# Whole tiled blocks, output stores from ScalarE, and ten early x in a four-layer graph kernel

## The chip, the core and the metric

The kernel runs on one core of a Trainium2 chip. The core has five engines with an instruction stream each: PE (TensorE, the matrix unit), DVE (VectorE), ACT (ScalarE), POOL (GpSimd) and SP (SyncE, which here only issues transfers). An instruction starts when the one before it on its engine is through and the semaphores it waits for are set; engines do not look past a waiting instruction. The metric is the device time of one execution in microseconds (us), less is better. The profile comes from one such execution.

## The reference, cut to what matters

The input `x` holds 128 independent batches of 128 nodes with 512 features (float32). Each batch goes through four layers, and after each one `x = layernorm(x + layer(x))`, without gain or bias:

```python
# 0: x1 = (adj @ x) @ W0 + bias0
# 1: h = x @ W;  e = leaky_relu(h@a1 [rows] + h@a2 [columns]) * adj
#    layer = elu(softmax(e) @ h + beta * h)
# 2: A = adj @ x;  layer[o] = max over columns of relu(A + b[o])
# 3: q, k, v = x @ w_qkv  (8 heads of 64)
#    o = softmax(q k^T / 8, masked where adj == 0) @ v,  then o @ w_proj + b_proj
#    layer = o + layernorm(o) * gamma + beta3
```

In layer 2 both weight matrices of the general form are `adj`, so the pairwise term falls away and the line above is what is left of it.

## The kernel before, in words

The work is planned in Python while the program is built. Each batch is a chain, a generator called `batch(i)` (L1009 in the profile's numbering), which asks for an engine with `yield use(engine, work, take, late, urgent, follow)`: how long it will need it, which buffers it takes, how much later the result is there. `Plan.run` (L161) always grants the request that could start first by these estimates; among equals, `follow` goes ahead of `urgent`, and that ahead of the rest, then the lower rank, which is the batch number less some head start. When a request is granted, the chain goes on and writes its instructions. So the order on every engine is fixed at build time by the planner's estimates; on the chip each engine only follows its list. A request counts as able to start when its engine is free and its buffers are given back (`at`, L126). `yield event` makes a chain wait without an engine.

Buffers are few. PSUM has eight banks, `ps`. In SBUF there are 21 buffers `t` of 512 columns, 15 `q` of 1024 and 7 `u` of 256. `CAPS` limits how many of them one use may hold: 8 `x`, 2 `xr`, 4 `yT` (all `t`), 4 `v`, 8 `qk` and 4 `xT` (all `q`).

Batches form groups of four (the last two groups have two). In order, a batch is loaded (`load`, L402), mixed by the adjacency (L300 for the first 12, L319 through a transposition by DVE and a round trip through DRAM `x_d` for the others), multiplied by W0 (L292), normalised, and given attention logits; `attention1` (L649) makes the attention weights of two batches at a time with two more round trips (`s_d`, `e_d`). Then come layer 1 (L300 with `u`, and seven half-size products per pair of batches instead of eight, L832), layer 2 (L1096) and a transposition through `x_d`. For a group of four, `section` (L860) makes q, k and v of all its batches, again in seven products each (L881). A batch that waits for its turn is spilled to DRAM (`x_s`, L998) and fetched again (L1006), since x buffers are short.

Two steps use the matrix unit in halves, the *tiled* steps. `score` (L952) makes the 8 heads' logits of one batch: eight matmuls over 64 rows, in pairs that run side by side, into two PSUM banks. The banks come free when DVE has added the mask to them (two instructions L1128). `attends` (L973) multiplies v by the transposed softmax: eight matmuls with 64 columns each into one bank, which comes free when ACT has copied it (L1192). `tiled` (L927) writes, for one group, its own four scores and the four attends of the group before. Three scores are one request that takes six banks; the fourth score and the four attends are single requests with `follow=True`. Between two requests other work on PE can be granted. The last `APART = 5` groups take no attends with them; these are requests of their own (`attend`, L965).

After `attends` a batch is projected (seven products per pair, L832; the last four batches with L292 or L1304), and `normed` (L1269) adds, normalises and stores it: the last step before the store is the activation L279 on ACT, and the store is issued by SP (L1287).

At the start `loads` (L431) issues adjacency, weights and the first x in a fixed order. Batches 0 to 7 have x buffers; `GUESTS = 6` more, 8 to 13, lie two each in the three first `v` buffers, which the first group doesn't need yet. The others wait for an x buffer.

Near the end, three numbers shift ranks: `LAST, AHEAD` move the last 14 batches 8 ranks ahead, and `SOON` moves the q, k, v and tiled requests of the last six groups ahead by up to 20.

Of the kernel before, what the change touches and what calls it, by code (L numbers as in the profile page):

```python
# [19 lines left out]
APART = 5  # L20
FIRST = 0
PAIRS = 2
SOON = 0,4,8,12,16,20
WHOLE = 2
KEPT = 4
ATTENDS = 2
# [1 line left out]
SEVEN1 = 1  # L28
SEVENP = 1
PLAIN = 4  # L30
GUESTS = 6
CLOSE = 2900
SOFT = 10
PROJ = 0
# [11 lines left out]

BUFS = {"ps": 8, "t": 21, "q": 15, "u": 7}
POOL = {"x": "t", "xr": "t", "yT": "t", "v": "q", "qk": "q", "xT": "q"}
CAPS = {"x": 8, "xr": 2, "yT": 4, "v": 4, "qk": 8, "xT": 4}
LAST,AHEAD = 14,8  # L50
DIRECT = 12
LATER = 2
LANDED = 4.0
# [15 lines left out]
class Plan:  # L69
# [9 lines left out]
    def __init__(self):  # L79
        self.free, self.requests = {}, []  # L80
        self.slots = {name: [0.0] * n for name, n in BUFS.items()}
        self.caps, self.held = {name: [0.0] * n for name, n in CAPS.items()}, {}
        self.now = 0.0

    def use(self, engine, work, take=None, late=0.05, urgent=False, follow=False):

        names = take if callable(take) else lambda: (take,) if take else ()
        return engine, work, names, late, 0 if follow else 1 if urgent else 2
# [4 lines left out]
    def done(self, event, late=0.0):  # L97
        event.left -= 1
        event.at = max(event.at, self.now + late)
        if not event.left:  # L100
            for r in event.chains:
                r["ready"] = max(r["ready"], event.at)
                self.step(r, None)

    def give(self, slot):
        name, i = slot
        self.slots[POOL.get(name, name)][i] = self.now
        if name in CAPS:
            self.caps[name][self.held.pop(slot)] = self.now
# [51 lines left out]
    def run(self):  # L161
        while self.requests:
            t, _, _, n = min(
                (self.at(r), r["want"][4], r["rank"], n) for n, r in enumerate(self.requests)
            )
            assert t < float("inf"), "the chains wait for each other"
            r = self.requests.pop(n)
            engine, work, take, late, _ = r["want"]
            self.free[engine] = t + work
            self.now = r["ready"] = t + work + late  # L170
            got = self.claim(take())
            self.step(r, got[0] if len(got) == 1 else got)
# [3 lines left out]
def gnn_stack_kernel(  # L176
# [17 lines left out]
    nc = tc.nc  # L194
    NB = x.shape[0]
# [5 lines left out]
    ps = ctx.enter_context(tc.tile_pool(name="ps", bufs=1, space=PSUM))  # L201

    plan = Plan()
    use, give, done = plan.use, plan.give, plan.done
# [197 lines left out]
    def load(i, engine="SP", queue=nc.sync):  # L402
        n = i - CAPS["x"]
        if 0 <= n < GUESTS:
            slot = yield use(engine, 0.5, () if n % 2 else "v")
            x_slot[i] = x_slot[i - 1] if n % 2 else slot
            if not n % 2:
                room[slot] = buf(slot, 2, D)
                guests[slot] = 2
            xs[i] = room[x_slot[i]][:, n % 2]  # L410
        else:
            x_slot[i] = yield use(engine, 0.5, "x")
            xs[i] = buf(x_slot[i], D)
        queue.dma_start(xs[i], x[i])
        landing(loaded[i], P)
# [15 lines left out]
    def loads():  # L431
        yield use("SP", 0.4)
        adj_slot.append((yield use("SP", 0.0, "t")))
        adj_sb = buf(adj_slot[0], D)[:, :P]
        adj_slot.append(adj_sb)
        nc.sync.dma_start(adj_sb, adj)
        landing(adj_in, P // 4)
        yield from load(0, "ACT", nc.scalar)
        w0_slot.extend((yield use("SP", 0.0, lambda: ("qk", "qk"))))
        halves = [buf(slot, 2, D) for slot in w0_slot]  # L440
        w0_nat.extend(halves[k // 2][:, k % 2] for k in range(K))
        for k in range(K):
            yield use("SP", 0.4)
            nc.sync.dma_start(w0_nat[k], w0[k * P : (k + 1) * P])
            landing(w0_chunk[k], P)
        yield from load(1)
        yield use("SP", 0.4)
        nc.sync.dma_start(bias0_sb, rows(bias0, D))
        landing(bias0_in, P)
        for i in range(2, 4):  # L450
            yield from load(i)
        slot = yield use("SP", 1.0, "qk")
        matrix(w1_sb, w1)
        a_sb = buf(slot, 2, D)
        nc.sync.dma_start(a_sb, rows(a, 2 * D).rearrange("p (s f) -> p s f", s=2))
        landing(w1_in, (K + 2) * P)
        plan.start(logit_rows(a_sb, slot), 0)
        for i in range(4, 8):
            yield from load(i)
        yield use("SP", 2.0)  # L460
        permuted(w0_sb, w0)
        landing(w0_in, K * P)
        yield use("SP", 1.0)
        nc.sync.dma_start(beta1_sb, rows(beta1, 1))
        nc.sync.dma_start(
            b2_sb, bass.AP(tensor=b2.tensor, offset=b2.offset, ap=[[1, P], [1, 1]])
        )
        landing(scalars_in, 2 * P)
        for i in range(8, CAPS["x"] + GUESTS):
            yield from load(i)  # L470
        yield use("SP", 2.5)
        permuted(wqkv_sb, w_qkv)
        matrix(wproj_sb, w_proj)
        for dst, src in ((bproj_sb, b_proj), (gamma_sb, gamma), (beta3_sb, beta3)):
            nc.sync.dma_start(dst, rows(src, D))
        landing(w3_in, (4 * K + 3) * P)
        plan.start(weight_sums(), 0)
        for i in range(CAPS["x"] + GUESTS, NB):
            yield from load(i)

    idle = []
# [140 lines left out]
    def soon(g):  # L622
        return SOON[g - len(sizes)] if g >= len(sizes) - len(SOON) else 0

# [302 lines left out]
    def tiled(gr, before, bs):  # L927
        yield gr.qk
        waiting = list(range(before.size)) if before else []
        for b in waiting:  # L930
            yield before.rows[b]

        now, later = bs[:3], bs[3:]
        slots = yield use(
            "PE", 0.45 + 0.87 * len(now) + (0.1 if waiting else 0),
            lambda: ("ps", "ps") * len(now), late=0.0, urgent=True,
        )
        for b in now:
            score(gr, b, slots[:2])
            slots = slots[2:]  # L940

        for n, b in enumerate(now):
            done(gr.scored[b], 0.15 - 0.87 * (len(now) - 1 - n))
        for b in later:
            slots = yield use("PE", 0.87, lambda: ("ps", "ps"), late=0.0, follow=True)
            score(gr, b, slots)
            done(gr.scored[b], 0.15)
        for b in waiting:
            slot = yield use("PE", 0.87, "ps", late=0.0, follow=True)
            attends(before, (b,), [slot])  # L950

    def score(gr, b, slots):  # L952

        p = [bank(slot, K, P) for slot in slots]
        qk = gr.qkT[b]
        for c in range(K):
            for j in range(2):
                rws = slice(j * HD, (j + 1) * HD)
                nc.tensor.matmul(
                    p[j][:, c, :], qk[rws, c, :], qk[rws, K + c, :],  # L960
                    start=True, stop=True,
                )
        gr.sc[b] = p, slots
# [9 lines left out]
    def attends(gr, bs, slots):  # L973
        for b, slot in zip(bs, slots):
            v, prT = gr.heads.pop(b)

            p = bank(slot, K, P)
            for c in range(K):
                for j in range(2):
                    nc.tensor.matmul(  # L980
                        p[j * HD : (j + 1) * HD, c, :],
                        v[:, (2 * c + j) * HD : (2 * c + j + 1) * HD],
                        prT[:, j * K + c], start=True, stop=True,
                    )
            give(gr.slot["qk", b])
            gr.o[b] = p, slot, v
        for n, b in enumerate(bs):
            done(gr.attended[b], 0.2 - 0.87 * (len(bs) - 1 - n))
# [280 lines left out]
    def normed(i, o, release, fetched):  # L1269

        added = yield from add_rows(o, fetched, i)
        xb = xs[i]
        mv, rstd = yield from mean_rstd(o)
        yield added
        b_t1 = yield use("DVE", 2.0, "t")
        t1 = buf(b_t1, D)
        nc.vector.scalar_tensor_tensor(  # L1277
            t1, o, mv[:, 0:1], gamma_sb, op0=ALU.subtract, op1=ALU.mult
        )
        total = row_sums()  # L1280
        nc.vector.scalar_tensor_tensor(  # L1281
            xb, t1, rstd, xb, op0=ALU.mult, op1=ALU.add, accum_out=total[0]
        )
        release()
        yield from layernorm_sums(xb, total, b_t1)
        yield use("SP", 0.5, late=3.0)
        nc.sync.dma_start(out[i], xb)  # L1287
        give(x_slot[i])

    def last(i, oT, v, release, biased):  # L1290
# [100 lines left out]
```

## Time and profile before

| | us |
|---|---|
| time, median of 3 runs | 3126.23 (3123.97 to 3129.34) |
| the profiled execution's own time | 3127.87 |
| its span, first to last instruction | 3126.1 |
| PE busy (matmuls) | 3022.6 |
| DVE busy | 2636.1 |
| ACT busy | 1939.0 |
| POOL busy | 1749.1 |

The span is 1.8 us below the time of its own execution and within 0.2 us of the median. "Busy" is the time in which at least one instruction of the engine runs; matmuls overlap in the records, so a busy PE may still run at half its clock. PEclk is the share of the clock that the chip granted to the matrix unit. A row of a wait view names the engine, the buffer and line that waited, what ended the wait, and then the sum, the count and the longest. A row of the timeline gives the start, the length, and the merged instructions with their count; a bracket at its end is the idle time before it and what ended that. A matmul of float32 shows as two records: a 128x512 output is 2 records, a 128x256 output likewise.

The transfers are 432.19 MB, nearly all on one queue, at 138 GB/s on average. SP issued 127 full output stores of 256 KB; the issue took 344 ns in the median.

### The profile page before, as it was taken

Reading aid. Unit: us, or ns where it says so; the run is one execution under the profiler, and the core shown is the slowest. Engines: PE = TensorE matmul, PEld = TensorE weight load, DVE = VectorE, ACT = ScalarE, POOL = GpSimd, SP = SyncE. Lnnn points to the kernel's source line nnn. Section 1 sums busy time; section 2 is a strip of 40 time slices with the busy share of each in tenths; the row PEclk is TensorE's granted clock in tenths of the full one; section 3 lists DMA queues with packets and bytes.
Section 4 is the critical chain, followed back from the end, with each engine's and each line's share of the span. In section 5 each row is a group of like instructions: output and inputs, shape, how many; then the busy total and the mean of one; then the engine's idle time right before and its main releaser. Section 6 shows DMA issues by size and latency. Waiting matters only on the chain. (4 is left out here: it accounts for less than half of the span.)

```text
span 3126.1 us, 51622 instructions
## 1 busy us (share of the span) xinstructions
PE 3022.6 (97%) x15807; PEld 2365.2 (76%) x15807; DVE 2636.1 (84%) x5749; ACT 1939.0 (62%) x5862; POOL 1749.1 (56%) x1814
## 2 busy tenths in 40 slices
PE   8899999999999999999999999999999999999996
PEld 5577787777877777777777777777777777677894
DVE  7878888888888898888988889888888888888876
ACT  4656666766656665667666567666666656655663
POOL 6544555665555664556565557545555655645644
PEclk9999999999999999999999999999999999999997
DMA  5355455554464554554555545545554545542453
GB/s 186 80 126 152 127 154 132 159 142 135 130 164 121 148 147 131 143 147 135 152 135 137 154 124 157 145 131 154 137 160 122 162 111 151 135 133 93 129 149 98
DMA packets 884948, 432.19 MB, mean 138 GB/s; under 512 B 572224, under 2 KB 785856, under 8 KB 884672
## 3 DMA queue, kind: packets, MB, share of 16 engines
q1 hardware_dynamic: 884528, 428.63, 49.6%
q8 instruction: 127, 2.08, 0.3%
q14 instruction: 149, 1.22, 0.1%
q10 hardware_dynamic: 144, 0.26, 0.0%
HBM read 223.15 MB, written 205.59 MB: 137 GB/s over the span
## 5 line engine op out<-in xcount | busy, mean ns | idle before, releaser
L243 POOL TENSOR_TENSOR sums<-sums,neghalf 128x1 f32<-128x1 f32 x383 | 263.2, 689 | 359.0 <-ACT sums L275 358.4
L292 PE MATMUL ps<-w_sb,t 128*128 128x512 f32 x928 | 423.9, 600 | 10.9 <-DMA t<-x_d 7.8
L1150 ACT ACTIVATE q<-q,nmx 128x128 f32<-128x128 f32 x1008 | 394.6, 394 | 34.4 <-DVE nmx L1136 34.3
L881 PE MATMUL ps<-q,wsum_sb 128*128 128x256 f32 (+1 forms) x1584 | 356.5, 374 | 4.6 <-POOL q L819 4.6
L881 PE MATMUL ps<-q,wqkv_sb 128*128 128x256 f32 (+1 forms) x1584 | 360.4, 373 | 0.0
L881 PEld LDWEIGHTS ps<-q,wsum_sb 128*128 128x128 f32 x1584 | 294.2, 191 | 57.1 <-issue 12.4
L881 PEld LDWEIGHTS ps<-q,wqkv_sb 128*128 128x128 f32 x1584 | 292.7, 190 | 51.9 <-issue 12.5
L292 PEld LDWEIGHTS ps<-w_sb,t 128*128 128x128 f32 x928 | 177.2, 193 | 191.7 <-issue 177.6
L243 POOL TENSOR_TENSOR n<-n,neghalf 128x1 f32<-128x1 f32 x257 | 174.1, 678 | 258.3 <-DVE n L238 231.4
L279 ACT ACTIVATE t<-t,sums 128x512 f32<-128x512 f32 x371 | 301.9, 814 | 12.4
L742 ACT COPY q<-ps 128x256 f32<-128x256 f32 (+1 forms) x483 | 178.6, 410 | 193.3 <-PE ps L881 114.7
L819 POOL TENSOR_TENSOR q<-q 128x256 f32<-128x256 f32 (+1 forms) x252 | 232.5, 928 | 85.7 <-PE ps L881 39.7
L754 DVE TENSOR_TENSOR q<-ps,q 128x256 f32<-128x256 f32 (+1 forms) x483 | 209.1, 467 | 83.3 <-PE ps L881 59.1
L273 ACT ACTIVATE t<-t,sums 128x512 f32<-128x512 f32 x249 | 178.7, 718 | 124.8 <-DVE sums L271 117.4
L285 POOL TENSOR_TENSOR t<-t,bproj_sb 128x512 f32<-128x512 f32 x124 | 178.8, 1447 | 135.0 <-ACT t L799 84.8
L285 POOL TENSOR_TENSOR t<-t,beta_sb 128x512 f32<-128x512 f32 x122 | 167.0, 1372 | 110.1 <-DVE t L1111 100.4
L742 ACT COPY t<-ps 128x256 f32<-128x256 f32 x378 | 138.5, 368 | 145.1 <-PE ps L832 133.1
L1045 DVE SCALAR_TENSOR_TENSOR t<-t,wa_rows 128x512 f32<-128x512 f32 x244 | 211.6, 869 | 15.2 <-ACT t L279 6.1
L754 DVE TENSOR_TENSOR t<-ps,t 128x256 f32<-128x256 f32 x378 | 155.1, 416 | 77.0 <-ACT t L742 35.4
L285 POOL TENSOR_TENSOR t<-t,t 128x512 f32<-128x512 f32 (+1 forms) x126 | 176.7, 1403 | 71.6 <-DMA t<-x_s 56.7
L832 PE MATMUL ps<-wsum_sb,t 128*128 128x256 f32 x768 | 199.5, 383 | 9.7 <-ACT t L742 9.7
L832 PE MATMUL ps<-w_sb,t 128*128 128x256 f32 x768 | 198.4, 383 | 1.6 <-DVE t L754 0.8
(164 smaller groups left out, 7381.7 us busy)
## 6 DMA issues: line engine op xcount, KB each, us to landing
p_d<-t SPq DMA_DIRECT2D x256, 256.0 KB
q<-p_d SPq DMA_DIRECT2D x128, 512.0 KB
x_d<-t SPq DMA_DIRECT2D x244, 256.0 KB
q<-x_d SPq DMA_DIRECT2D x512, 64.0 KB
out<-t SPq DMA_DIRECT2D x127, 256.0 KB
t<-x_s SPq DMA_DIRECT2D x124, 256.0 KB
t<-in_x SPq DMA_DIRECT2D x121, 256.0 KB
x_s<-t SPq DMA_DIRECT2D x118, 256.0 KB
```

What stands on the lines that cost most here:

```text
L243: nc.gpsimd.tensor_tensor(rstd, ve, neghalf, op=ALU.pow)
L273: nc.scalar.activation(buf_or_bank(unread), xb, AF.Square, bias=nm, accum_out=squares)
L279: nc.scalar.activation(xb, xb, AF.Identity, bias=nmr, scale=rstd)
L285: nc.gpsimd.tensor_tensor(dst, dst, other, op=ALU.add)
L292: nc.tensor.matmul(p, lhs(k), rhs(k), start=(k == 0), stop=(k == K - 1))
L742: nc.scalar.copy(c, a)
L754: nc.vector.tensor_tensor(c, a, c, op=ALU.add)
L819: nc.gpsimd.tensor_tensor(blocks(out), blocks(a), blocks(b), op=ALU.subtract)
L832: nc.tensor.matmul(p, t[:, k], w[:, k, :], start=first and k == 0, stop=final and k == 1, skip_group_check=True,)
L881: nc.tensor.matmul(to, lhs, rhs, start=first and j == 0 and k == 0, stop=final and k == 1, skip_group_check=True,)
L1045: nc.vector.scalar_tensor_tensor(unread, xb, 1.0, wa_rows[:, j, :], op0=ALU.mult, op1=ALU.mult, accum_out=gr.s[:, b, j : j + 1],)
L1150: nc.scalar.activation(pr[:, j, :], pr[:, j, :], AF.Exp, bias=nmx[:, j : j + 1], accum_out=sums[:, j : j + 1],)
```

## The change

Six edits, all in the planner's input, with the same arithmetic:

1. The output store of every batch but the last is issued by ACT, right after the activation that made its data (`follow=True`), not by SP. The last batch's two half stores stay on SP.
2. `tiled` writes steps of two batches: two scores, then the attends of the group before two at a time, then the other two scores. Each step is one request, `urgent`, and all but the first also `follow`.
3. In `Plan.run`, a `follow` request on PE counts as 0.6 us earlier than it could start (`STICK`) when the next one is chosen, so that it wins against work that could start up to 0.6 us sooner.
4. Ten batches instead of six are early guests (8 to 17): two each in four `v` buffers and one `xT` buffer. The last four are loaded after the layer-3 weights.
5. `yT` may hold six buffers, not four.
6. `LAST` is 16 and `SOON` is 0, 0, 4, 8, 12, 16.

```diff
-SOON = 0,4,8,12,16,20
+SOON = 0,0,4,8,12,16
-GUESTS = 6
+GUESTS = 10
+ROOMS = ["v"] * 4 + ["xT"] * 2 + ["qk"] * 5
+STICK = 0.6
-CAPS = {"x": 8, "xr": 2, "yT": 4, "v": 4, "qk": 8, "xT": 4}
-LAST,AHEAD = 14,8
+CAPS = {"x": 8, "xr": 2, "yT": 6, "v": 4, "qk": 8, "xT": 4}
+LAST,AHEAD = 16,8
...
     def run(self):
             t, _, _, n = min(
-                (self.at(r), r["want"][4], r["rank"], n) for n, r in enumerate(self.requests)
+                (self.at(r) - (STICK if r["want"][0] == "PE" and not r["want"][4] else 0.0),
+                 r["want"][4], r["rank"], n) for n, r in enumerate(self.requests)
             )
             r = self.requests.pop(n)
+            t = self.at(r)
...
     def load(i, engine="SP", queue=nc.sync):
-            slot = yield use(engine, 0.5, () if n % 2 else "v")
+            slot = yield use(engine, 0.5, () if n % 2 else ROOMS[n // 2])
...
     def tiled(gr, before, bs):
-        now, later = bs[:3], bs[3:]
-        slots = yield use(
-            "PE", 0.45 + 0.87 * len(now) + (0.1 if waiting else 0),
-            lambda: ("ps", "ps") * len(now), late=0.0, urgent=True,
-        )
-        for b in now:
-            score(gr, b, slots[:2])
-            slots = slots[2:]
-
-        for n, b in enumerate(now):
-            done(gr.scored[b], 0.15 - 0.87 * (len(now) - 1 - n))
-        for b in later:
-            slots = yield use("PE", 0.87, lambda: ("ps", "ps"), late=0.0, follow=True)
-            score(gr, b, slots)
-            done(gr.scored[b], 0.15)
-        for b in waiting:
-            slot = yield use("PE", 0.87, "ps", late=0.0, follow=True)
-            attends(before, (b,), [slot])
+        steps = [(score, bs[:2])]
+        steps += [(attends, waiting[b : b + 2]) for b in range(0, len(waiting), 2)]
+        steps += [(score, bs[b : b + 2]) for b in range(2, len(bs), 2)]
+        was = None
+        for do, batches in steps:
+            n = len(batches)
+            slots = yield use(
+                "PE", 0.87 * n + (0.45 if was is None else 0.15 if was is not do else 0),
+                lambda: ("ps",) * (n if do is attends else 2 * n),
+                late=0.0, urgent=True, follow=was is not None,
+            )
+            was = do
+            if do is attends:
+                attends(before, batches, slots)
+                continue
+            for m, b in enumerate(batches):
+                score(gr, b, slots[2 * m : 2 * m + 2])
+                done(gr.scored[b], 0.15 - 0.87 * (n - 1 - m))
...
     def normed(i, o, release, fetched):
-        yield use("SP", 0.5, late=3.0)
-        nc.sync.dma_start(out[i], xb)
+        yield use("ACT", 0.4, late=3.0, follow=True)
+        nc.scalar.dma_start(out[i], xb)
```

In the built programs PE has the same 7917 matrix instructions before and after, and the other engines the same compute instructions; only their order differs, and 127 stores stand in ACT's list and not in SP's. The four steps of the block stand as follows, in batches (S a score, A an attend; a bar is other work in between):

| | S3 / S1 A4 | S4 A4 | S2 A4 S2 | S2 / A4 S2 | others |
|---|---|---|---|---|---|
| before, of the blocks with attends | 21 | 7 | 0 | 0 | 0 |
| after | 0 | 0 | 23 | 5 | 0 |

In full, the change of the matrix unit's form takes place at these places: before, 55 times from whole to score, 11 from whole to attend, 30 from score to attend, 1 from attend to score, and 66 back to whole; after, 35, 17, 24, 28 and 52.

## The prediction

> **What bounds the kernel now.** I read the page's busy shares first, then busy time by stage, then PE's waits in the middle stage, then the timeline around the tiled blocks.
>
> The page says that PE is the bound and that the other engines have room on average:
>
> ```profile
> PE 3022.6 (97%) x15807; PEld 2365.2 (76%) x15807; DVE 2636.1 (84%) x5749; ACT 1939.0 (62%) x5862; POOL 1749.1 (56%) x1814
> ```
>
> Busy time by stage (length, then each engine, then PEclk, the granted clock):
>
> ```profile
> 60.00:180.00 120.00, 97.54 (x381) 68.80 (x380) 109.66 (x259) 70.61 (x174) 82.28 (x84) 0.90 0.41 110
> 180.00:2640.00 2460.00, 2426.06 (x12677) 1907.54 (x12676) 2097.52 (x4611) 1565.65 (x4766) 1372.39 (x1430) 1.00 0.51 140
> 2640.00:2920.00 280.00, 262.59 (x1361) 205.22 (x1360) 236.26 (x498) 167.75 (x513) 158.00 (x162) 0.97 0.47 126
> 2920.00:3070.00 150.00, 150.00 (x1090) 132.71 (x1090) 115.92 (x217) 89.11 (x304) 72.06 (x78) 1.00 0.48 139
> 3070.00:3126.10 56.10, 28.87 (x94) 17.11 (x90) 36.87 (x76) 18.93 (x42) 26.30 (x27) 0.70 0.27 89
> ```
>
> PE idles 22.5 us in the second row, 33.9 in the third, 17.4 in the fourth, 27.2 in the last (8.7 of it after the last matmul), 2.5 before 60 us: 103.5, which is 3126.1 - 3022.6. The last row and the first shown also have a slowed clock. Taking the usual distance between ends of neighbouring records (429 ns for 512 columns, 216 for 256, 54 in the tiled steps) as full-speed work gives 2935 us; changes of form cost 35 (below), idle 103.5, and 52 are left, most of it slow clock: 13 in 60 to 180, 17 in the long middle, 10 in 2640 to 2920, 9 at the end. So at most some 155 us are to be had, and the change can only move these.
>
> In the middle stage the waits are few, and those for banks lead:
>
> ```profile
> PE ps L980 <- DVE q L1128: 4.1, 1, 4.1
> PE ps L319 <- DVE q L1128: 3.4, 1, 3.4
> ...
> PE ps L959 <- DVE t L322: 2.9, 1, 2.9
> ```
>
> With four smaller rows for L1128 (2.5, 2.3, 2.0, 0.6) that is 17.8 of the 33.9; 3.7 more stand in 2640 to 2920. One of them, PE first, then what DVE did:
>
> ```profile
> 1774.22 2.95 PE L959 MATMUL ps<-q 64*128 64x128 f32 x48
> 1780.53 1.34 PE L319 MATMUL ps<-t,adjT 128*128 128x512 f32 x2 [3.37 <-DVE q L1128]
> ```
>
> ```profile
> 1778.08 0.42 DVE L673 TENSOR_TENSOR u<-u,s 128x256 f32<-128x256 f32 x1 [4.00 <-DMA u<-s_d]
> ...
> 1779.80 3.07 DVE L1128 TENSOR_TENSOR q<-ps,maskb 128x512 f32<-128x512 f32 x5
> ```
>
> Three scores hold six of eight banks. DVE, whose next instruction is L673, waits for a row that SP issued late, behind twelve x_d reads of 0.63 us; the mask additions queue behind it, and PE has no bank.
>
> **The Trainium skill.** "TensorEngine Tiling (Array Packing)", section Key Properties: a change of tiling mode drains the array. The trace agrees: neighbouring ends are 303 ns apart from whole to score (249 more than 54), 253 to attend (199 more), 413 back to a 256-column matmul (197 more than 216). "TensorE: Matmul & The Clock Gate", Part 1: after an idle window of about 3.4 us the clock drops to half. The trace agrees: slow stretches of 3.4 us or its multiples follow most idle stretches above 1.7 us. "DMA: Bandwidth & Descriptors", Issuing engines are not separate DMA queues: another issuer saves only issue time. No run here has shown that yet.
>
> **The change part by part.**
>
> *Changes of form.* Before: 55 x 0.249 + 11 x 0.199 + 30 x 0.199 + 1 x 0.249 + 66 x 0.197 = 35.1 us. After: 35 x 0.249 + 17 x 0.199 + 24 x 0.199 + 28 x 0.249 + 52 x 0.197 = 34.1. Gain 1.0 us: whole blocks save re-entries, but alternating inside costs nearly the same. The "whole" of the change is worth almost nothing by itself.
>
> *Banks.* A score pair now takes four banks at once, not six; its two-score successor needs four again, when all eight are held (four scores, four attends). Between them lie four attends, 64 records x 54 ns + 0.2 = 3.7 us of cover. Matching score ends and L1128 ends in the trace, DVE finished the second score's banks 1.6 to 7.2 us after that score (median 3.0) over 29 groups. The excess over 3.7 sums to about 15 us in ten groups, three over 2 us. Before, these stalls are 17.8 + 3.7 = 21.5 us, six of them 1.66 or more. So 6 us of idle and some 4 of slow clock: 10 us. After the block the attends' banks serve PE next; ACT's copies L1192 mostly started 0.05 to 0.9 us after their attend, so this adds none. Bounds: nothing stalls (-30); DVE late by 2 us more in each of 28 blocks (+40 with clock).
>
> *Early x.* The four guests move 4 x (0.86 L319 + 3.44 L292) = 17.2 us of PE work ahead, into the stage with 22.5 us idle and 13 of slow clock. Its waits are round trips (x_d 7.2, e_d 6.6) and L742 (6.1), the serial steps of a lone pair, which extra products can cover; the built order sets four L292 products between them. SP pays 4 x 0.35, moved earlier behind the weights. Gain 14 of 36; from 25 down to -5, if the fourth v buffer then comes free late.
>
> *Stores.* SP loses 127 x 0.344 = 43.7 us of issue and the waits in front of them, 294.5 us in all (208.1 after L279, the rest behind other ACT work). Cover already there: in the stall above SP was not at a store but in x_d reads. ACT gains 127 x 0.40 (its one issue took 403 ns) = 51 us, with 1187 idle; each must wait for the activation just ahead of it and holds what follows on ACT, copies L742 among it, by 0.4 to 0.5. PE's waits for ACT are some 32 us in 26 waits, so even 0.5 more on each is 13. I take -1; bounds -6 and +13.
>
> *The end.* Before, the last score ends at 3062.7 and the span 63.4 later. After it PE had 10.4 us of work before the first last-group projection; now it is 16.4 (15 half-size pair steps of 0.86 and four attends), so the last score is reached 6 us earlier. DVE's list from the first of its last four L1128 sums to 45.8 us by row medians before, 49.4 after, both under 63.4: latency, not throughput. Now both last softmaxes stand together, ahead of the leftover normalisations. Their DVE steps and the few between sum to about 20 us, the p_d round trip adds 7; both attends come 28 us after the score, not 27.5 and 43. Two projections (6.9 us), then 12.4 us of DVE after the last products begin to be read (before 5.4) and 4 of ACT and POOL: 28 + 1 + 7 + 12 + 4 is 52; with a slow clock and waits 60. That is 3 more: 9 us, bounds +6 and -16.
>
> *yT, LAST, SOON, STICK* only re-order. Nothing in the trace prices them; 0, bounds +-12 around the 27 us lost in 2640 to 2920.
>
> Sum: -1 -10 -14 -1 -9 = -35. A new order has waits of its own: those not for banks, 16 us in the long stage, are the pattern; I add half, 8. -27 or -28 from the span 3126.1, which is the median within 0.2: **3098 us**, 0.9% faster. Its own range is 3076 to 3116.
>
> **The rivals.**
>
> *Nothing moves* (0.08): the head is bound by DVE (109.66 of 120 busy), so the extra products only push the waits back, and the rest cancels. For it: that row. Against: DVE's share in the other stages is as high as 0.85 without such stalls. 3120 to 3132, say 3125.
>
> *Second scores wait for DVE* (0.14): slower. In a whole block all eight banks are out, and no other work can be slipped in on PE's list. If DVE's fourth L1128 is late by a further 1.5 us on average, 28 x 1.5 = 42 us idle, and a slow window of 1.7 us loss in half of them, 24: 66 - 25 of the other gains = +41 at 3167. It decides from about 0.6 us further lateness on. For it: L673 stands close ahead of the first L1128 in four after-blocks. Against: the four L1128 stand back to back in half of the new DVE lists. I take 3145 as its time.
>
> *Stores on ACT hold PE* is the 13 us above; alone it doesn't turn the sign.
>
> *The blocks are not whole:* excluded, 23 of 28 are in the built order.
>
> **How the numbers follow.** The forecast's case has 0.78. Measurement tells 0.2%, 6 us, from no change. Faster 0.78, same 0.08, slower 0.14. The range 3072 to 3136 leaves out a tenth of the slow side and less than a tenth of larger gains.
>
> **What would show it.** Idle PE in 60 to 180 falls from 22.5 to about 12, with PEclk above 0.9; PE's waits for L1128 fall below 15 us and stand on L959; changes of form stay at 34 us; stores appear as ACTq issues near 0.4 us, with ACT busy about as before; the last stage has less than 20 us of idle PE. It is wrong if L959 waits for L1128 over 30 us, if waits for L742 or L279 grow over 15, or if 2640 to 2920 loses over 40.

## The result, and the profile after

The changed kernel takes 3090.77 us, median of four runs (3088.57 to 3096.97), the kernel before in the same comparison 3125.1 (3121.87 to 3129.34): ratio 0.9893, interval 0.9873 to 0.9912, 1.1% faster. The forecast was 3098 with 3072 to 3136. The profiled execution took 3088.57 us, its span 3086.8; the span before was 3126.1, so 39.3 us are to be explained.

The page's busy shares, first part, of the changed kernel:

```profile
PE 2998.5 (97%) x15807; PEld 2348.9 (76%) x15807; DVE 2613.3 (85%) x5749; ACT 1941.5 (63%) x5862; POOL 1749.0 (57%) x1814
```

The instructions are the same in number, and so is the work; PE's busy time still fell by 24 us, because busy matmuls at a slow clock are longer. Busy time by stage of the changed kernel (stretch and length, then PE, PEld, DVE, ACT, POOL, then PEclk, DMA share, GB/s):

```profile
60.00:180.00 120.00, 108.60 (x446) 74.83 (x445) 116.41 (x271) 77.66 (x197) 92.14 (x92) 1.00 0.48 121
180.00:2640.00 2460.00, 2411.87 (x12680) 1897.99 (x12680) 2094.77 (x4628) 1564.62 (x4756) 1373.43 (x1429) 1.00 0.51 141
2640.00:2920.00 280.00, 276.74 (x1525) 223.72 (x1522) 229.32 (x502) 178.98 (x556) 159.90 (x168) 0.99 0.49 133
2920.00:3086.80 166.80, 143.82 (x947) 119.08 (x945) 132.99 (x256) 93.25 (x293) 85.10 (x90) 0.94 0.40 124
```

PE's idle time in the rows is now 11.4, 48.1, 3.3 and 23.0 us. Before it was 22.5, 33.9 and 17.4 in the first three. So the start and the stretch before the end won, and the long middle lost 14.

Stretches of time do not hold the same work in two kernels, so for the account I cut by work. For every matmul record I took the distance of its end from the end before it, less the full-speed spacing of its shape (429, 216, 111 or 54 ns) and the price of a change of form; what is left is loss, as an idle wait or as a slow clock. The cuts lie at 5, 85 and 94% of the 2935.4 us of full-speed work:

| loss, us | first 5% | 5 to 85% | 85 to 94% | last 6% | after the last matmul | forms | span |
|---|---|---|---|---|---|---|---|
| before | 40.0 | 51.0 | 27.6 | 26.7 | 8.7 | 35.1 | 3126.1 |
| after | 15.9 | 68.7 | 5.5 | 6.8 | 18.9 | 34.1 | 3086.8 |
| difference | -24.1 | +17.7 | -22.1 | -19.9 | +10.2 | -1.0 | -39.3 |

Of the losses in the first four columns idle waits were 93.4 before and 68.0 after, slow clock 52.0 and 29.0. That slow windows go with idle ones is what "TensorE: Matmul & The Clock Gate", Part 1, of the Trainium skill says of idle windows of about 3.4 us. Here each us of idle carried another 0.4 to 0.6 of slow matmuls. In the two traces together each of the 11 idle stretches above 3.4 us meets a slow one (one that lies over its end or begins within 3.5 us of it). Of the 21 between 1.7 and 3.4 us, 12 do: 11 of 14 before, 1 of 7 after. So the prediction's "most idle stretches above 1.7 us" held for the kernel before (18 of 21) and not for the changed one (5 of 11).

*The start.* One of PE's waits there in the kernel before, at a product of an x (L292):

```profile
74.92 5.23 PE L292 MATMUL ps<-w_sb,t 128*128 128x512 f32 x8 [3.35 <-DMA t<-x_d]
```

Timeline of PE between 60 and 110 us in the changed kernel, three rows of its products L296 (the line was L292):

```profile
74.13 3.67 PE L296 MATMUL ps<-w_sb,t 128*128 128x512 f32 x8 [1.95 <-DMA t<-x_d]
...
86.66 3.67 PE L296 MATMUL ps<-w_sb,t 128*128 128x512 f32 x8 [1.10 <-DVE u L683]
...
93.07 3.67 PE L296 MATMUL ps<-w_sb,t 128*128 128x512 f32 x8
```

The extra products stand between the steps of the first attention pairs, and the gaps left there are 1 to 2 us.

*The middle.* PE's waits between 180 and 2640 us in the changed kernel (engine, buffer and line that waited, what ended it; sum, times, longest):

```profile
PE ps L885 <- ACT q L746: 6.6, 3, 3.7
PE ps L984 <- DVE q L1132: 6.2, 4, 4.2
PE ps L304 <- DMA u<-e_d: 5.6, 4, 3.7
PE ps L836 <- ACT t L746: 5.4, 5, 1.7
PE ps L1100 <- ACT t L283: 5.1, 4, 2.9
...
PE ps L836 <- DVE q L1132: 1.3, 1, 1.3
...
PE ps L296 <- DVE q L1132: 0.2, 1, 0.2
```

The mask addition, now L1132, ends 7.7 us of waits here and 8.2 in the whole trace. Before it was 14.9 and 18.6; the 17.8 and 21.5 of the prediction have 2.9 behind L322 with them, the transposition of a mixed row, which frees a bank too. That line, now L326, ends 3.9 us of waits after. The waits of this stretch that don't end with the mask addition rose from 19.0 to 40.4. What can hold PE up is seen around the longest wait for the mask addition. PE first:

```profile
1369.23 2.06 PE L963 MATMUL ps<-q 64*128 64x128 f32 x32
...
1372.19 1.89 PE L885 MATMUL ps<-wsum_sb,q 128*128 128x256 f32 x8
1378.24 5.09 PE L984 MATMUL ps<-q,q 128*64 128x128 f32 x46 [4.16 <-DVE q L1132]
```

Then DVE in the same stretch:

```profile
1374.02 0.85 DVE L677 TENSOR_TENSOR u<-u,s 128x256 f32<-128x256 f32 x1 [6.55 <-DMA u<-s_d]
1374.90 1.37 DVE L681 SCALAR_TENSOR_TENSOR u<-u 128x256 f32<-128x256 f32 x1
...
1377.50 2.47 DVE L1132 TENSOR_TENSOR q<-ps,maskb 128x512 f32<-128x512 f32 x4
...
1380.67 0.42 DVE L681 SCALAR_TENSOR_TENSOR u<-u 128x256 f32<-128x256 f32 x1
```

And the issues of SP, from a little earlier:

```profile
1357.90 6.02 SPq L345 DMA_DIRECT2D q<-x_d  x8
...
1364.68 2.54 SPq L345 DMA_DIRECT2D q<-x_d  x4
1367.32 0.57 SPq L666 DMA_DIRECT2D s_d<-s  x1
1367.93 2.54 SPq L345 DMA_DIRECT2D q<-x_d  x4
1370.58 0.56 SPq L671 DMA_DIRECT2D u<-s_d  x1
```

This is one of the five blocks that aren't whole (two scores, other work, then the attends). The attends have no bank, since the four mask additions stand behind L677 on DVE; L677 waits 6.55 us for its row, whose issue stands behind sixteen x_d reads on SP. No store is left on SP, and the chain that the prediction showed in the kernel before is still there. DVE's waits for that row rose from 37.5 us in the whole trace to 63.9.

*The end.* PE's two longest waits from 3070 us on in the kernel before:

```profile
PE ps L980 <- DMA q<-p_d: 7.1, 2, 4.5
PE ps L292 <- ACT q L1192: 4.7, 1, 4.7
```

Timeline of PE in the last 47 us of the changed kernel:

```profile
3053.38 1.09 PE L984 MATMUL ps<-q,q 128*64 128x128 f32 x16 [1.51 <-DMA q<-p_d]
3055.96 1.97 PE L984 MATMUL ps<-q,q 128*64 128x128 f32 x16 [1.48 <-DMA q<-p_d]
3058.97 5.42 PE L296 MATMUL ps<-wproj_sb,q 128*128 128x512 f32 x8 [1.04 <-ACT q L1196]
3064.23 3.62 PE L1308 MATMUL ps<-wproj_sb,q 128*128 128x256 f32 x16
```

The last score ends at 3026.9 (before 3062.7). From there to the end of the span it is 59.9 us, before 63.4; the last two attends start 26.4 and 29.0 us after it, before 27.5 and 43.1. Other projections fill PE until 3052, so the last matmul comes 40.9 us after the score and not 54.6, but 18.9 us of normalisation are left behind it in place of 8.7.

### The profile page after: what moved, and what is told of

Same layout as the page of the kernel before. It is cut to its first block, busy times and chain, and to the rows that moved or that the text cites. A ratio compares the mean times of both kernels' runs of the same rounds, so it can differ in the third digit from the quotient of the medians.

```text
span 3086.8 us, 51622 instructions
## 1 busy us (share of the span) xinstructions
PE 2998.5 (97%) x15807; PEld 2348.9 (76%) x15807; DVE 2613.3 (85%) x5749; ACT 1941.5 (63%) x5862; POOL 1749.0 (57%) x1814
## 5 line engine op out<-in xcount | busy, mean ns | idle before, releaser
L296 PE MATMUL ps<-w_sb,t 128*128 128x512 f32 x928 | 419.5, 595 | 12.0 <-DMA t<-x_d 4.0
L1154 ACT ACTIVATE q<-q,nmx 128x128 f32<-128x128 f32 x1008 | 394.6, 394 | 36.4 <-DVE nmx L1140 35.8
L885 PEld LDWEIGHTS ps<-q,wsum_sb 128*128 128x128 f32 x1584 | 295.3, 191 | 64.3 <-issue 16.4
L296 PEld LDWEIGHTS ps<-w_sb,t 128*128 128x128 f32 x928 | 175.5, 191 | 193.7 <-issue 173.6
L283 ACT ACTIVATE t<-t,sums 128x512 f32<-128x512 f32 x363 | 295.4, 814 | 12.1
L746 ACT COPY q<-ps 128x256 f32<-128x256 f32 (+1 forms) x483 | 178.5, 411 | 134.1 <-PE ps L885 127.5
L746 ACT COPY t<-ps 128x256 f32<-128x256 f32 x378 | 138.4, 368 | 194.0 <-PE ps L836 154.3
L277 ACT ACTIVATE t<-t,sums 128x512 f32<-128x512 f32 x245 | 175.8, 718 | 104.3 <-DVE sums L275 98.7
L758 DVE TENSOR_TENSOR t<-ps,t 128x256 f32<-128x256 f32 x378 | 155.0, 415 | 66.2 <-PE ps L836 27.3
L289 POOL TENSOR_TENSOR t<-t,t 128x512 f32<-128x512 f32 (+1 forms) x126 | 177.9, 1414 | 34.3 <-issue 13.4
```

The source lines that it names most:

```text
L277: nc.scalar.activation(buf_or_bank(unread), xb, AF.Square, bias=nm, accum_out=squares)
L283: nc.scalar.activation(xb, xb, AF.Identity, bias=nmr, scale=rstd)
L289: nc.gpsimd.tensor_tensor(dst, dst, other, op=ALU.add)
L296: nc.tensor.matmul(p, lhs(k), rhs(k), start=(k == 0), stop=(k == K - 1))
L746: nc.scalar.copy(c, a)
L758: nc.vector.tensor_tensor(c, a, c, op=ALU.add)
```

## The experiments

All leave the arithmetic as it is. The table has the times, then the loss by work as above (forms and the 1.4 us ahead of the first matmul left out). The times are medians, the losses come from one profiled execution each. The changed kernel's was its fastest of four (3088.57) and e4's its slowest (3100.08). They have one order on PE and differ in the issuer of the stores alone, and so do the kernel before and e1. These two pairs are 11.4 and 6.4 us apart in the column 5 to 85%, and 0.8 at most in the others. So a few us in that column say nothing.

| run | us | before, us | ratio and interval | first 5% | 5 to 85% | 85 to 94% | last 6% | after last |
|---|---|---|---|---|---|---|---|---|
| e1_stores_in_place | 3123.27 | 3127.18 | 0.9989 (0.9982 to 0.9996) | 40.7 | 44.6 | 26.8 | 27.3 | 8.7 |
| e2_before_other_order | 3159.11 | 3127.18 | 1.0106 (1.0091 to 1.0121) | 35.8 | 84.0 | 27.7 | 28.2 | 8.7 |
| e3_after_other_order | 3139.11 | 3127.18 | 1.0042 (1.0027 to 1.0058) | 17.0 | 78.9 | 37.1 | 26.4 | 9.1 |
| e4_after_stores_on_sp | 3098.55 | 3127.18 | 0.9906 (0.9887 to 0.9925) | 16.5 | 80.1 | 5.5 | 6.4 | 18.9 |
| e5_before_ten_guests | 3208.93 | 3123.44 | 1.028 (1.0265 to 1.0295) | 38.8 | 138.3 | 21.4 | 26.1 | 8.7 |
| e6_after_six_guests | 3120.62 | 3123.44 | 0.999 (0.9981 to 0.9999) | 36.8 | 55.9 | 25.4 | 16.7 | 12.2 |
| e7_before_end_ranks | 3126.02 | 3123.44 | 1.0011 (1.0003 to 1.0018) | 40.2 | 44.9 | 27.7 | 30.4 | 9.1 |
| e8_after_old_end_ranks | 3115.2 | 3123.44 | 0.9975 (0.9967 to 0.9982) | 16.8 | 64.0 | 6.8 | 49.8 | 9.1 |
| e9_before_guests_and_yT | 3123.71 | 3125.96 | 0.9995 (0.9986 to 1.0003) | 16.7 | 90.6 | 23.0 | 13.5 | 9.6 |
| e10_after_four_yT | 3124.16 | 3125.96 | 0.9991 (0.9984 to 0.9997) | 35.7 | 28.4 | 40.9 | 33.7 | 8.9 |
| e11_after_split_blocks | 3147.04 | 3125.96 | 1.0068 (1.0052 to 1.0083) | 16.9 | 92.7 | 33.8 | 26.8 | 9.1 |
| e12_after_sp_price | 3050.35 | 3125.96 | 0.9758 (0.9743 to 0.9772) | 23.3 | 9.8 | 18.7 | 14.7 | 8.7 |

### e1_stores_in_place: the kernel before, stores issued by ACT, order kept

```diff
     def normed(i, o, release, fetched):
         yield use("SP", 0.5, late=3.0)
-        nc.sync.dma_start(out[i], xb)
+        nc.scalar.dma_start(out[i], xb)
```

The planner's request stays as it was, so PE's, DVE's and POOL's lists don't change.

> The kernel before with its planned order on every engine kept; only the 127 full output stores are issued by ACT at the place in program order where SP issued them. Theory (the gain comes from where PE waits for x at the start, for banks, and at the end): ratio to before within 0.998 to 1.002, since SP's waits at the stores end no wait of PE. Rival A (the stores held SP back, and SP's freed 44 us of issue and 294 us of waiting are the gain): 0.995 or less, and PE's waits for transfers (u, t from x_d, q from p_d; 28 us in sum) fall by more than 10 us. Rival B (issue on ACT delays copies): over 1.003.

Ratio 0.9989, some 3.4 us: the move is worth a tenth of a per cent by itself, and rival A, in which the stores are the gain, falls. It is also not the loss of up to 13 us that was bounded.

### e4_after_stores_on_sp: the changed kernel with the stores back on SP, order kept

```diff
         yield use("ACT", 0.4, late=3.0, follow=True)
-        nc.scalar.dma_start(out[i], xb)
+        nc.sync.dma_start(out[i], xb)
```

> The changed kernel with its planned order, the 127 stores issued by SP at the same places in program order. Theory: as the changed kernel within 0.2%, ratio to before 0.987 to 0.992. Rival A: half of the gain or more is lost, 0.995 or more, since SP, which was planned without them, waits for ACT at each store.

0.9906 against 0.9893 with overlapping intervals: again about a tenth of a per cent, and not told from nothing. The profile of the changed kernel has the stores, listed by their line (engine, operation, ns least/median/most, first and last start), at

```profile
L1291 ACTq DMA_DIRECT2D out<-t x127: 338/338/382, 343.7 to 3083.6; - x127
```

0.338 us each where SP took 0.344. "DMA: Bandwidth & Descriptors", section Issuing engines are not separate DMA queues, of the Trainium skill says that another issuer saves issue time only; both runs agree. The issue time that SP is rid of, 43.7 us over the span, is not where SP stands in the way.

### e2_before_other_order and e3_after_other_order: the same kernels, the planner's order drawn again

```diff
-MARGIN = 1.0
+MARGIN = 1.05
```

`MARGIN` is how long after its inputs a request on PE counts as able to start, where it doesn't follow. 50 ns more has no meaning for the chip; it makes the planner decide some ties otherwise, and from there on the orders differ.

> The kernel before with one planner constant moved that means nothing by itself: MARGIN 1.05 instead of 1.0. The order on all engines is planned anew. Theory: a new order alone moves the time by up to 10 us either way, ratio 0.997 to 1.003. Rival C (the gain is a lucky order and no part matters): it moves by 20 us or more, under 0.994 or over 1.006.

> The changed kernel with MARGIN 1.05 instead of 1.0, a new order again. Theory: ratio to before 0.986 to 0.993, all parts still being there. Rival C: anywhere from 0.985 to 1.003, so that 0.996 or more speaks for it.

My theory, at most some 10 us, fell. The kernel before came out 33 us slower and the changed kernel 48 (1.0042 against 0.9893), each by a 50 ns constant. That is as much as the whole change brings, and rival C, luck of the order, has its number. The planner of each kernel, run by itself, shows that much of the luck is in the plan: its last step ends at 3063.6 us in the kernel before and 3128.5 in e2, at 3030.6 in the changed kernel and 3077.8 in e3. The middle of e2:

```profile
180.00:2640.00 2460.00, 2403.42 (x12509) 1880.77 (x12508) 2080.26 (x4565) 1547.78 (x4718) 1357.29 (x1413) 0.99 0.51 139
```

PE idles 56.6 us there, and 33.9 in the kernel before, with nothing changed. So a comparison of two kernels that were planned anew says little of an edit; what can be asked is which stage moves the same way in every order. The first 5% did: 17.0 in e3 too, 35.8 in e2.

### e5, e6, e9, e10: who makes the start faster

e5_before_ten_guests: the kernel before with the changed kernel's ten early x, and nothing else.

```diff
-GUESTS = 6
+GUESTS = 10
+ROOMS = ["v"] * 4 + ["xT"] * 2 + ["qk"] * 5
...
-            slot = yield use(engine, 0.5, () if n % 2 else "v")
+            slot = yield use(engine, 0.5, () if n % 2 else ROOMS[n // 2])
```

> The kernel before with the ten early x alone (GUESTS 10, the same places and load order as in the changed kernel). Theory D (the early x fill the start, whatever the rest of the order): idle and slow PE in the first 5% of the matrix work falls from 40 us (before; 36 in its other order) to 13 to 20. The whole time moves by that and by the luck of a new order, which has shown +33 and +48 us here: ratio 0.985 to 1.012. Rival E (the start was a lucky order too): 30 us or more in the first 5%.

The start still loses 38.8 us, as rival E said, though not for its reason, as e9 shows. Theory D, that the early x alone make the gain, fell, by this stage's row:

```profile
60.00:180.00 120.00, 97.35 (x349) 62.04 (x348) 106.23 (x257) 69.06 (x175) 75.34 (x77) 0.90 0.41 106
```

It is the row of the kernel before (97.54 busy, PEclk 0.90) with four more x lying ready. The 2.8% by which e5 is slower stands in the middle (138.3).

e6_after_six_guests: the changed kernel with six early x.

```diff
-GUESTS = 10
-ROOMS = ["v"] * 4 + ["xT"] * 2 + ["qk"] * 5
+GUESTS = 6
...
-            slot = yield use(engine, 0.5, () if n % 2 else ROOMS[n // 2])
+            slot = yield use(engine, 0.5, () if n % 2 else "v")
```

> The changed kernel with six early x as before. Theory D: idle and slow PE in the first 5% of the matrix work goes from 16 us back to 33 to 42. Rival E: it stays under 25. Whole time 0.992 to 1.015 of before.

36.8: without the extra guests the gain is gone, so they are needed, and something besides.

e9_before_guests_and_yT: e5 with six `yT`.

```diff
-CAPS = {"x": 8, "xr": 2, "yT": 4, "v": 4, "qk": 8, "xT": 4}
+CAPS = {"x": 8, "xr": 2, "yT": 6, "v": 4, "qk": 8, "xT": 4}
```

> The kernel before with ten early x and six yT buffers together, nothing else. Theory H (the start needs both: early x to work on and yT buffers to hold their mixed rows; the ten x alone left the first 5% at 39 us): the first 5% of the matrix work loses 14 to 20 us, and PE's order there is that of the changed kernel. Rival I (the start needs the whole block form or ACT's stores too): 30 us or more. Whole time with the luck of the order: 0.98 to 1.015.

16.7, as in the changed kernel, with no other part of the change. The row again:

```profile
60.00:180.00 120.00, 108.41 (x439) 74.62 (x438) 115.66 (x268) 77.56 (x196) 91.84 (x92) 0.99 0.46 118
```

e10_after_four_yT: the changed kernel with four `yT`, the reverse of that edit.

> The changed kernel with four yT buffers, all else kept. Theory H: the first 5% loses 33 to 42 us again. Rival J (yT does nothing, e5 failed for another reason): 14 to 20. Whole time 0.99 to 1.03; e5, with the same two settings, had 1.028.

35.7, and the row of the start is back:

```profile
60.00:180.00 120.00, 95.92 (x361) 62.67 (x360) 107.09 (x259) 69.52 (x176) 75.56 (x77) 0.93 0.42 106
```

Theory H held: the two parts have to come together. Over all the kernels here, the first 5% lose 15.9 to 23.3 us with both (after, e3, e4, e8, e9, e11, e12) and 35.7 to 40.7 with one or none (before, e1, e2, e5, e6, e7, e10), whatever the order. A mixed batch's x_d read takes a `yT` buffer before its product can run (L325 in the kernel before), so more x without more `yT` stop one step further on. The traces agree: up to 110 us SP issued 8 of these reads, four to a batch, in the kernel before and in e6, 12 in e5, 14 in e10, and 24 in e9 and the changed kernel. Beside the stores' tenth of a per cent this is the one part of the gain that is not a draw. By itself it doesn't show in the time: e9 has it and is at 0.9995, since its middle loses 90.6.

### e7_before_end_ranks and e8_after_old_end_ranks: the last groups' ranks

```diff
-SOON = 0,4,8,12,16,20
+SOON = 0,0,4,8,12,16
-LAST,AHEAD = 14,8
+LAST,AHEAD = 16,8
```

e7 makes this edit in the kernel before, e8 takes it back in the changed kernel.

> The kernel before with LAST 16 and the new SOON alone. Theory F (the gain at the end is the order that came out, not these ranks): loss of PE in the last 15% of the matrix work, with the time after the last matmul, stays within 52 to 80 us (before 63, other order 65, changed 31, its other order 73). Rival G (the ranks make it): 45 us or less. Ratio 0.99 to 1.015.

> The changed kernel with LAST 14 and the old SOON. Theory F: the last 15% lose 45 to 80 us, like the changed kernel's other order (73), not the 31 of the changed kernel. Rival G would have the same here, so e7 tells them apart; under 40 would say that ranks do nothing at all. First 5%: 14 to 19 us, as the guests are kept. Ratio 0.99 to 1.01.

From 85% of the work on, with what follows the last matmul, e7 loses 67.2 us (before 63.0): the ranks alone bring nothing. e8 loses 65.7 where the changed kernel loses 31.2, but its 85 to 94% is still low (6.8), so that stage's gain doesn't come from the ranks. Nor do the ranks hold the last stage down: e3 and e11 have the new ones and lose 72.6 and 69.7 over the same stretch. What the changed kernel gains after 85% belongs to the order that came out, the ranks being one of several things that pick it. Which property of that order it is was not tried.

### e11_after_split_blocks: the changed kernel with the old `tiled`

```diff
-        steps = [(score, bs[:2])]
-        steps += [(attends, waiting[b : b + 2]) for b in range(0, len(waiting), 2)]
-        steps += [(score, bs[b : b + 2]) for b in range(2, len(bs), 2)]
...
+        now, later = bs[:3], bs[3:]
...
```

`STICK` is taken out with it.

> The changed kernel with tiled blocks as before (three scores, one score, attends one by one, no STICK). Theory K (whole blocks take PE's waits for DVE's mask additions down to about half): waits of PE that end with L1128 of the kernel before are 14 us or more, as in before and its relatives (19, 17, 11, 36, 10), where whole blocks have had 8, 15, 10, 2, 11; yet the long middle (5% to 85% of the work) loses no more than with whole blocks: 40 to 80 us. Rival L (whole blocks are where the gain is): the middle loses over 85. Ratio 0.985 to 1.01.

Waits ended by the mask addition are 11.3 us, less than the 14 that K, that whole blocks cut these waits, wanted to see. The middle's 92.7 meets the number of L, that whole blocks are where the gain is. But with split blocks the middle lost as little as 44.6 (e1), and with whole ones as much as 80.1 (e4), so one order can't tell. Over the orders that were made, these waits sum to 0, 1.5, 3.9, 8.2, 9.2, 10.1 and 14.7 us with whole blocks, mean 6.8, and 9.7, 11.0, 11.3, 17.0, 17.6, 18.6 and 35.5 with split ones, mean 17.2. They differ by 10 on average and overlap; two of each seven are one and the same order. So a saving of that size is likely and not shown. Blocks alone in the kernel before were not tried.

### e12_after_sp_price: the changed kernel, planned with SP's own price

The timeline above shows four x_d reads taking SP 2.54 us. The planner counts 2.0 for them. The theory: SP falls behind the plan wherever they crowd, and the short rows of the attention weights, due at a planned time, come late.

```diff
-        b1 = yield use("SP", 2.0, "yT", late=LANDED)
+        b1 = yield use("SP", 2.6, "yT", late=LANDED)
...
-            got = yield use("SP", 2.0, lambda: () if j in gr.xT else ("xT",))
+            got = yield use("SP", 2.6, lambda: () if j in gr.xT else ("xT",))
```

> The changed kernel with the planner's price for four reads of x_d on SP at 2.6 us, which is what the trace shows, instead of 2.0. Theory M (the middle loses PE time since SP is later than planned): PE's waits for transfers in the middle fall below 10 us, and the ratio to before is 0.985 or less. Rival C (a new order is a draw): ratio anywhere in 0.985 to 1.01.

Ratio 0.9758 (0.9743 to 0.9772): 76 us faster than the kernel before, and 1.4% under the changed kernel (0.9758 / 0.9893). The middle of e12:

```profile
180.00:2640.00 2460.00, 2448.11 (x12927) 1932.57 (x12926) 2121.77 (x4696) 1600.44 (x4834) 1403.36 (x1459) 1.00 0.53 143
```

and PE's waits in it that are over 1 us:

```profile
PE ps L304 <- DMA u<-e_d: 3.1, 2, 2.4
PE ps L836 <- ACT t L746: 2.4, 1, 2.4
PE ps L296 <- DMA t<-x_d: 2.4, 1, 2.4
```

PE idles 11.9 us there, not 48.1. No wait for the mask addition is left, DVE's waits for the row from s_d fall to 21.0 us in the whole trace (63.9), and the middle loses 9.8 by work, where every other kernel here lost 28 to 138. Theory M's numbers came. One of its signs tells nothing: PE's waits for transfers are 5.5 us here, but at 9.5 they were below 10 in the changed kernel too.

Is it again a draw? The planner speaks against it. Its plan for e12 ends at 3056.0 us, 25 later than that for the changed kernel, and the chip was through 8.6 us ahead of it. In all thirteen other kernels the chip ended 24.5 to 67.7 us behind the plan (56.2 in the changed kernel). So e12 didn't draw a shorter plan; it has one that the chip keeps. Two things stay open. This is one order with the new price, and a second was not run. And the edit makes the planner expect the data of these reads 0.6 us later as well as SP busy for longer; which of the two counts was not tried. Its first 5% (23.3) and its last parts are no better than others'; the gain is in the stage that the theory named.

## Why the prediction was right, and where it was not

The time was forecast at 3098 and is 3090.77. By the terms of the sum, against the differences by work:

- *Changes of form*, -1.0: counted in the trace with the same prices, -1.0.
- *Early x*, -14 with bounds -25 and +5: measured -24.1 in the first 5%, near the bound. The mechanism is right, the size is off: idle PE between 60 and 180 us fell by 11.1, to 11.4, as said (about 12), but the slow clock there went nearly whole, PEclk 0.90 to 1.00, some 11 us and not the few that were counted. And the step missed its condition: `yT` was priced at nothing as "only re-orders", while e5 and e10 show that the gain needs it.
- *Banks*, -10: waits ended by the mask addition fell by 10.4 us (18.6 to 8.2), by 9.4 with those behind L322, now L326; 6 of idle were counted. They were to stand on the scores and now stand on the attends (L984, 6.7 of 8.2). e11 doesn't show that the blocks did it.
- *Stores*, -1: e1 measured some -3, e4 the same within its interval. The bound of +13 was not needed.
- *A new order's own waits*, +8: this is the step that failed most. Waits that don't end with the mask addition rose by 21.4 us in the long stage, and the middle lost 17.7 in all, with the banks' saving in it. It was taken as half of what the old order had; e2 and e3 show that a redraw moves the total by 33 to 48 us. The prediction saw SP's x_d reads ahead of a late row, and took them as the place of one stall, not as a standing error of the plan; e12, one order, speaks for the latter.
- *The end*, -9: measured -9.7 (last 6% and what follows the last matmul). Score to end was to take 60 us and takes 59.9, the attends 28 us after the score and start at 26.4 and 29.0. But e8 and e3 show that this end is a property of one order, not of the edit.
- *yT, LAST, SOON, STICK*, 0 within 12: 85 to 94% gave -22.1, beyond the bound. e7 and e8 show that the ranks aren't its cause.

So the sum came within 7 us of the median, 11 of the profiled span, because errors of both signs cancelled: -10 in the start and -22 before the end against +20 or so in the middle. Of the rivals, second scores waiting for DVE did not come about (its own sum, +41, gave 3167; the 3145 put down for it has no working). "Nothing moves" with DVE as the start's bound is refuted by the first row: DVE went from 109.66 to 116.41 busy of 120 and PE still won 11 us. The rival that was missing is the one that e2 and e3 measured, that a new order by itself is worth a per cent either way. The plan itself would have told of the draw: from the kernel before to the changed one its end moves by -33.0 us, and -34.3 was measured. It can't be trusted so far in general: the plan of e6 is 29.6 us longer than that of the kernel before, and e6 ran 2.8 us shorter. With this rival the range would have been wider on the slow side: e2's constant alone, put into the changed kernel, gives 3139, outside it.

Of the signs that were to show it, the idle time of the start, the clock, the forms, the stores at 0.338 us and L283 came as told; L746, once L742, ends 12.0 us of PE's waits in the middle and 16.4 in the whole trace, where it was 12.8, so it didn't grow by 15; the last stage has 23.0 us of idle PE, not under 20, since 18.9 of it now follow the last matmul.

## What to carry to other kernels

Where a planner fixes the order, an edit is measured together with a new draw of the order, and here a constant without meaning was worth as much as the six edits: compare stage by stage, and against orders drawn again, before an edit gets the credit. Compare the end of the plan with the end on the chip, too: the first tells much of what the draw brought, the difference what the plan has wrong. Give the planner the durations that the trace shows, above all for the issues of a queue that many short transfers share; in the one order made so, that was worth more than all six edits. Where two buffers limit one chain, as here at the start, raising either alone may bring nothing, and its trial then says nothing against both together.

## What the runs showed of the hardware that was not expected

An x_d read costs its issuer 0.63 us, in the median of 512, though a full store of 256 KB costs 0.34. The bytes alone don't set it: of two writes of 256 KB, that to x_d costs 0.33 us in the median and that to p_d 0.58.

The same DVE instruction with two inputs in SBUF takes very different times. In the timeline of DVE above L681 takes 1.37 us at 1374.90 and 0.42 at 1380.67. POOL in the timeline of the changed kernel:

```profile
1374.66 1.32 POOL L823 TENSOR_TENSOR q<-q,q 128x512 f32<-128x512 f32 x1
1375.95 0.90 POOL L823 TENSOR_TENSOR t<-t 128x256 f32<-128x256 f32 x1
...
1383.12 0.73 POOL L823 TENSOR_TENSOR u<-q 128x256 f32<-128x256 f32 x1 [4.86 <-ACT q L1196]
```

POOL subtracts two SBUF operands during the first and is idle during the second. Over the trace, 40 records of L681 have a mean of 425 ns with POOL's two-input instructions covering 31% of their time, and 24 have 1178 ns with 85% covered; L677 has 440 (34%) and 943 (99%). "SBUF — State Buffer", section Who interferes with whom, of the Trainium skill says that a DVE instruction with two SBUF inputs contends with a GpSimd instruction that reads SBUF, for ports that are an exclusive lock. The trace fits that, but it is an association: no run here took POOL's work away.
